# A graph layer on one core: masks moved to GpSimd as a no-edge comparison, and the pair loop put in a fixed issue order

## The chip, the cores and the metric

One core of a Trainium2 chip. The metric is the device time of one execution in microseconds (us). "Before" and "after" are the kernel before and after the change. Engines carry the names of the profile: PE is TensorE, PEld its weight loads, DVE is VectorE, ACT is ScalarE, POOL is GpSimd, SP is SyncE. The experiments ran in four batches on three chips; the kernel before, run beside each batch, had medians of 459.6 to 461.2 us.

## The reference, cut to what matters

Two graph layers over 3327 nodes with 64 features and a dense adjacency of zeros and ones. Layer 0 visits all pairs of nodes; layer 1 wants, for every edge, how many edges of the same row come after it (only the last 100 count, each with half the weight of the next).

```python
adj_att = jax.nn.sigmoid(left[:, None] + right[None, :] + b_att[0]) * adj
x_local = logmap(x[:, None, :], x[None, :, :], c)
support_t = jnp.einsum('ij,ijd->id', adj_att, x_local)
...                                     # layer 1
mask = (adj != 0).astype(support.dtype)
rank = jnp.cumsum(mask, axis=1)
deg = rank[:, -1:]
k = jnp.minimum(deg, float(MAX_NEIGH))
pos = rank - (deg - k)
w = mask * jnp.where(pos > 0, DECAY ** (k - pos), 0.0)
out = w @ support + bias
```

## The kernel before

The node axis is padded to 26 blocks of 128. A strip is 8, 8, 6 or 4 blocks of targets; for each strip the kernel runs over the 26 source blocks `j` from the last to the first, in rounds of at most 1024 columns. In a round, VectorE makes a 16-bit mask of the adjacency (`ad`), PE's triangular matmuls add it to running counters in PSUM (`pc`; SBUF and PSUM are the two memories in which the kernel's tiles lie, and its matmuls write to tiles in PSUM), and ScalarE or VectorE reads the counters out as bytes (`behind`). Beside this runs the pair work: tanh of `left + right`, the sigmoid product with `ad`, the pair matmuls into `pq`, two Gelus as a stand-in for the artanh of layer 0, the last product, and a matmul that adds the round to the strip's sums `po`.

```python
ad = work.tile([P, FMAX], F32, name="ad", bufs=4)
nc.sync.dma_start(ad[:, :span]..., adj_t[...])
mask = work.tile([P, FMAX], BF16, name="mask", bufs=3)
V.tensor_scalar(mask[:, :span], ad[:, :span], 0.0, None, op0=ALU.not_equal)
for j in js:
    now = part(mask, j)
    for f0, f1 in hv:
        if before is not None:
            T.matmul(pc[:, f0:f1], ca, before[:, f0:f1], ...)
        T.matmul(pc[:, f0:f1], cb, now[:, f0:f1], ...)
    before = now
    kept = behind(j)[:, i0 : i0 + F]
    if j % (2 if b0 == 0 else 4):
        A.activation(kept, pc[:, :F], AF.Relu)
    else:
        V.tensor_scalar(kept, pc[:, :F], 0.0, None, op0=ALU.max)
sg = work.tile([P, FMAX], F32, name="sg", bufs=3)
for j in js:
    A.activation(part(sg, j), left_b[:, :F], AF.Tanh, bias=right[:, j : j + 1], scale=0.5)
V.scalar_tensor_tensor(sg[:, :span], sg[:, :span], 1.0, ad[:, :span], op0=ALU.add, op1=ALU.mult)
pq = ps.tile([P, FMAX], F32, name="pq", bufs=2)
...                                     # pair matmuls into pq
s = work.tile([P, FMAX], F32, name="s", bufs=3)
A.activation(s[:, :span], pq[:, :span], AF.Gelu, scale=-WG / QS)
A.activation(s[:, :span], s[:, :span], AF.Gelu, scale=WH)
V.scalar_tensor_tensor(s[:, :span], s[:, :span], WD, sg[:, :span], op0=ALU.add, op1=ALU.mult)
for j in js:
    ...                                 # T.matmul(po, hw, s)
    next(steps, None)                   # one step of the per-node chain of the strip before
```

The per-node chain (`post`) closes layer 0 for the nodes of a finished strip, and it makes the rows that layer 1 multiplies. It is a row of VectorE instructions. In this kernel the order of each engine's queue is left to the scheduler.

Of the kernel before, what the change touches and what calls it, by code (L numbers as in the profile page):

```python
# [11 lines left out]
F32 = mybir.dt.float32  # L12
# [10 lines left out]
P = 128  # L23
# [5 lines left out]
STRIPS = [(0, 8), (8, 8), (16, 6), (22, 4)]  # L29
FMAX = 8 * P  # L30
JH = 13

GSTRIPS = [(0, 7), (7, 7), (14, 6), (20, 6)]
GFMAX = 7 * P
# [30 lines left out]


HS = 1024.0
CNT = 127.0


def halves(n):
# [364 lines left out]
def fast(ctx, tc, x, adj_t, r, w_att, b_att, weight, bias, out, flag):  # L436
# [27 lines left out]
    def column(value, name):  # L464
# [8 lines left out]
    id16 = const.tile([P, P], F16, name="id16")  # L473
    G.tensor_copy(id16, ident)

    cb = const.tile([P, P], BF16, name="cb")
    ca = const.tile([P, P], BF16, name="ca")
    G.memset(ca, -1.0)
    G.affine_select(out=cb, in_=ca, compare_op=ALU.is_gt, fill=0.0, base=0,
                    pattern=[[-1, P]], channel_multiplier=1)  # L480
    G.affine_select(out=cb, in_=cb, compare_op=ALU.not_equal, fill=CNT, base=0,
                    pattern=[[-1, P]], channel_multiplier=1)
    G.tensor_sub(ca, ca, cb)
    row1 = const.tile([1, P], BF16, name="row1")
    G.memset(row1, 1.0)
    rowc = const.tile([1, 512], BF16, name="rowc")
    G.memset(rowc, MAX_NEIGH - CNT)

    node = const.tile([P, NB], F32, name="node")
    G.memset(node, 1.0)  # L490
# [34 lines left out]
    behind_hi = const.tile([P, NB - JH, NP], U8, name="behind_hi")  # L525
    s2 = const.tile([P, NB, 2, D], F16, name="s2")

    post_pool = ctx.enter_context(tc.tile_pool(name="post", bufs=1))
    pairs = ctx.enter_context(ExitStack())
    ps = pairs.enter_context(tc.tile_pool(name="ps", bufs=1, space=PSUM))  # L530

    with tc.tile_pool(name="pre", bufs=1) as pre:
# [102 lines left out]
        V.tensor_mul(right, plr[:, :, 1], yr)  # L635
        V.tensor_scalar(right, right, batt, 0.5, op0=ALU.add, op1=ALU.mult)


        wn, opx = small("wn"), small("opx")
        V.tensor_scalar(wn, nrm, WA / 2, None, op0=ALU.mult)  # L640
# [16 lines left out]
    def behind(j):  # L657
        return behind_lo[:, j] if j < JH else behind_hi[:, j - JH]

    def in_range():  # L660

        st = post_pool.tile([P, 4], F32, name="st")
        t1 = post_pool.tile([P, NB], F32, name="st1")
        V.tensor_mul(t1, nrm, node)
        V.tensor_reduce(st[:, 0:1], t1, AX.X, ALU.max)
        V.scalar_tensor_tensor(t1, x2, c_c, t1, op0=ALU.mult, op1=ALU.mult)
        V.tensor_reduce(st[:, 1:2], t1, AX.X, ALU.max)
        V.tensor_mul(t1, bal, node)
        V.tensor_reduce(st[:, 2:3], t1, AX.X, ALU.max)
        V.tensor_reduce(st[:, 3:4], t1, AX.X, ALU.min)  # L670
        V.tensor_scalar(st[:, 3:4], st[:, 3:4], -1.0, None, op0=ALU.mult)
        pf = ps.tile([P, P], F32, name="pq", bufs=2)
        T.transpose(pf[:4, :], st, ident)
        st2 = post_pool.tile([4, 1], F32, name="st2")
        V.tensor_reduce(st2, pf[:4, :], AX.X, ALU.max)
        pf = ps.tile([P, P], F32, name="pq", bufs=2)
        T.transpose(pf[:1, :4], st2, ident[:4, :4])
        st3 = post_pool.tile([1, 4], F32, name="st3")
        V.tensor_copy(st3, pf[:1, :4])
        ok = post_pool.tile([1, 2], F32, name="ok")  # L680

        V.tensor_mul(ok, st3[:, 0:4:2], st3[:, 1:4:2])
        V.tensor_scalar(ok[:, 0:1], ok[:, 0:1], QMAX / 2, None, op0=ALU.is_le)
        V.tensor_scalar(ok[:, 1:2], ok[:, 1:2], 0.0, None, op0=ALU.is_equal)
        V.tensor_mul(ok[:, 0:1], ok[:, 0:1], ok[:, 1:2])
        V.tensor_scalar(flag, ok[:, 0:1], -1.0, 1.0, op0=ALU.mult, op1=ALU.add)
# [95 lines left out]
        V.tensor_sub(s2[:, bs, 1], w, s2[:, bs, 0])  # L782


    steps = iter(())
    for b0, nb in STRIPS:
        F = nb * P
        i0 = b0 * P
        hv = halves(F)
        blocks = slice(b0, b0 + nb)  # L790
        queue = nc.scalar if b0 == 0 else nc.sync

        iz = strip.tile([P, 8, P], F16, name="iz")[:, :nb]
        iu = strip.tile([KB, 8, P], F16, name="iu")[:, :nb]
        queue.dma_start(iu[:D], ju[:D, blocks])
        queue.dma_start(iu[D:], ju[KB : KB + 7, blocks])
        queue.dma_start(iz[:D], jz[D:, blocks])
        queue.dma_start(iz[D:], jz[:D, blocks])
        izf, iuf = iz.rearrange("p b q -> p (b q)"), iu.rearrange("p b q -> p (b q)")
        pc = ps.tile([P, FMAX], F32, name="pc")  # L800
        po = ps.tile([P, FMAX], F32, name="po")
        pl = ps.tile([P, FMAX], F32, name="pq", bufs=2)
        for b in range(nb):
            T.transpose(pl[:, b * P : (b + 1) * P], left[:, b0 + b : b0 + b + 1].to_broadcast([P, P]), ident)
        left_b = strip.tile([P, FMAX], F32, name="left_b", bufs=1)
        A.copy(left_b[:, :F], pl[:, :F])
        for f0, f1 in hv:
            T.matmul(pc[:, f0:f1], row1, rowc[:, : f1 - f0], start=True, stop=True, skip_group_check=True)

        per = FMAX // F  # L810
        before = None
        for hi in range(NB, 0, -per):
            lo = max(hi - per, 0)
            js = range(hi - 1, lo - 1, -1)
            span = (hi - lo) * F

            def part(t, j, a=0, b=F):
                return t[:, (j - lo) * F + a : (j - lo) * F + b]

            ad = work.tile([P, FMAX], F32, name="ad", bufs=4)  # L820
            nc.sync.dma_start(ad[:, :span].rearrange("p (b f) -> p b f", f=F),
                              adj_t[lo * P : hi * P, i0 : i0 + F].rearrange("(b p) f -> p b f", p=P))
            mask = work.tile([P, FMAX], BF16, name="mask", bufs=3)
            V.tensor_scalar(mask[:, :span], ad[:, :span], 0.0, None, op0=ALU.not_equal)  # L824
            for j in js:
                now = part(mask, j)
                for f0, f1 in hv:
                    if before is not None:
                        T.matmul(pc[:, f0:f1], ca, before[:, f0:f1], start=False, stop=True, skip_group_check=True)  # L829
                    T.matmul(pc[:, f0:f1], cb, now[:, f0:f1], start=False, stop=True, skip_group_check=True)  # L830
                before = now
                kept = behind(j)[:, i0 : i0 + F]
                if j % (2 if b0 == 0 else 4):
                    A.activation(kept, pc[:, :F], AF.Relu)  # L834
                else:
                    V.tensor_scalar(kept, pc[:, :F], 0.0, None, op0=ALU.max)  # L836


            sg = work.tile([P, FMAX], F32, name="sg", bufs=3)
            for j in js:  # L840
                A.activation(part(sg, j), left_b[:, :F], AF.Tanh, bias=right[:, j : j + 1], scale=0.5)  # L841
            V.scalar_tensor_tensor(sg[:, :span], sg[:, :span], 1.0, ad[:, :span], op0=ALU.add, op1=ALU.mult)  # L842

            pq = ps.tile([P, FMAX], F32, name="pq", bufs=2)
            for j in js:
                for f0, f1 in hv:
                    T.matmul(part(pq, j, f0, f1), ju[:KB, j, :], iuf[:, f0:f1], start=True, stop=False)  # L847
                    T.matmul(part(pq, j, f0, f1), jz[:, j, :], izf[:, f0:f1], start=False, stop=True)  # L848
            s = work.tile([P, FMAX], F32, name="s", bufs=3)
            A.activation(s[:, :span], pq[:, :span], AF.Gelu, scale=-WG / QS)  # L850
            A.activation(s[:, :span], s[:, :span], AF.Gelu, scale=WH)  # L851
            V.scalar_tensor_tensor(s[:, :span], s[:, :span], WD, sg[:, :span], op0=ALU.add, op1=ALU.mult)  # L852
            for j in js:
                for f0, f1 in hv:
                    T.matmul(po[: D + 1, f0:f1], hw[:, j, :], part(s, j, f0, f1), start=j == NB - 1, stop=j == 0)  # L855
                next(steps, None)
        for _ in steps:
            pass

        ot = work.tile([P, FMAX], F32, name="s", bufs=3)[: D + 1]  # L860
        V.tensor_copy(ot[:, :F], po[: D + 1, :F])
        pa = ps.tile([P, FMAX], F32, name="pq", bufs=2)
        for b in range(nb):
            c0 = (b // 4) * 512 + (b % 4) * (D + 1)
            T.transpose(pa[:, c0 : c0 + D + 1], ot[:, b * P : (b + 1) * P], ident[: D + 1, : D + 1])
        agg = post_pool.tile([P, 8, D + 1], F32, name="agg", bufs=2)
        for c in range(0, nb, 4):
            n = min(4, nb - c)
            A.copy(agg[:, c : c + n], pa[:, c * P : c * P + n * (D + 1)].rearrange("p (b d) -> p b d", b=n))
        steps = post(agg[:, :nb], b0, nb)  # L870
        if b0 == 0:
            in_range()
    pairs.close()


# [4 lines left out]
    with tc.tile_pool(name="l1", bufs=2) as l1, tc.tile_pool(name="l1_ps", bufs=1, space=PSUM) as l1_ps:  # L880
# [16 lines left out]
        for j in range(late):  # L897
            wt = decode(j)
            for n in range(len(chunks)):
                add(j, wt, n)  # L900
            for _ in range(2):
                next(steps, None)
        for _ in steps:
            pass
        weights = [decode(j) for j in range(late, NB)]
# [70 lines left out]
```

## Time and profile before

| | before |
|---|---|
| time, first three runs | 461.72 us median (459.25 to 464.87) |
| busy share PE, DVE, ACT, POOL | 82, 89, 80, 3 % |
| pair loop (first sigmoid to last copy of the sums) | 343.6 us of 459.1 |
| strips 0 to 3, by the prediction's cuts | 96.5, 104.1, 85.5, 57.5 us |

The lines themselves are in the prediction. Each has an engine, its line of the program, an operation, and what it wrote from what; "mean ns" is one instruction's duration, and neighbours on one engine overlap a little, so a duration of 1.22 us means one every 1.13 us. The figure after an arrow is the idle time that this releaser ended.

### The profile page before, as it was taken

What the parts mean: (1) busy time and instruction counts of PE and PEld (TensorE: products, weight loads), DVE (VectorE), ACT (ScalarE), POOL (GpSimd) and SP (SyncE); (2) the same over time, 40 slices, a digit from 0 to 9 for tenths busy, and PEclk for the clock granted to TensorE, in tenths of its full rate; (3) what the DMA queues carried; (4) which work ended last, traced back from release to release, by engine and by line L of the source; (5) the groups of instructions that cost most, each with busy time, mean ns of one, the idle gap of its engine ahead of it and who ended that gap; (6) DMA issues with size and microseconds to landing.
All of it is one profiled execution on the core that took longest, in us unless ns stands there. A gap on an engine that the chain in (4) does not pass through costs nothing.

```text
span 459.1 us, 4660 instructions
## 1 busy us (share of the span) xinstructions
PE 378.4 (82%) x1484; PEld 153.4 (33%) x1484; DVE 407.1 (89%) x774; ACT 369.2 (80%) x423; POOL 13.3 (3%) x30
## 2 busy tenths in 40 slices
PE   0266699999989799999997999889778897699293
PEld 0035233333323233333333444434322332244152
DVE  3895689999988999999998999999999998999821
ACT  1445989999894999999995999999599995888310
POOL 6000000000000000001000000020000000000000
PEclk9997699999999999999999999999999998899877
DMA  7103354545541444444442444344533420000003
GB/s 201 62 1 72 105 168 143 141 151 163 167 135 46 133 143 140 137 137 137 137 127 75 136 137 140 106 128 125 168 93 111 121 89 1 1 1 1 0 0 82
DMA packets 22840, 47.77 MB, mean 104 GB/s; under 512 B 8652, under 2 KB 9082, under 8 KB 22808
## 3 DMA queue, kind: packets, MB, share of 16 engines
q1 hardware_dynamic: 20522, 46.47, 34.7%
q10 hardware_dynamic: 2062, 0.87, 0.9%
q0 software_dynamic: 224, 0.07, 0.3%
q8 instruction: 13, 0.21, 0.2%
q14 instruction: 19, 0.16, 0.1%
HBM read 45.22 MB, written 0.85 MB: 100 GB/s over the span
## 4 chain that ended last, share of the span: by engine, by line

## 5 line engine op out<-in xcount | busy, mean ns | idle before, releaser
L855 PE MATMUL po<-s,hw 128*65 128x512 f32 (+1 forms) x364 | 165.3, 576 | 11.5 <-DVE s L852 11.1
L842 DVE SCALAR_TENSOR_TENSOR sg<-sg,ad 128x1024 f32<-128x1024 f32 (+1 forms) x91 | 103.5, 1141 | 7.5 <-ACT sg L841 7.3
L852 DVE SCALAR_TENSOR_TENSOR s<-s,sg 128x1024 f32<-128x1024 f32 (+1 forms) x91 | 104.8, 1152 | 3.7 <-ACT s L851 3.6
L841 ACT ACTIVATE sg<-left_b,right 128x1024 f32<-128x1024 f32 (+2 forms) x104 | 102.7, 1001 | 0.1
L851 ACT ACTIVATE s<-s 128x1024 f32<-128x1024 f32 (+1 forms) x91 | 91.4, 1006 | 0.1
L850 ACT ACTIVATE s<-pq 128x1024 f32<-128x1024 f32 (+1 forms) x91 | 87.7, 969 | 2.6 <-PE pq L848 2.6
L829 PE MATMUL pc<-mask,ca 128*128 128x512 bf16 (+1 forms) x175 | 65.7, 375 | 17.3 <-DVE behind_hi L836 7.2
L855 PEld LDWEIGHTS po<-s,hw 128*65 128x65 f32 x364 | 45.2, 138 | 98.9 <-issue 52.7
L847 PE MATMUL pq<-iu,ju 71*128 71x512 f16 (+1 forms) x182 | 67.8, 374 | 11.6 <-ACT s L850 11.6
L830 PE MATMUL pc<-mask,cb 128*128 128x512 bf16 (+1 forms) x182 | 66.7, 376 | 5.3 <-DVE mask L824 5.1
L848 PE MATMUL pq<-iz,jz 128*128 128x512 f16 (+1 forms) x182 | 66.6, 371 | 0.0
L824 DVE TENSOR_SCALAR mask<-ad 128x1024 bf16<-128x1024 f32 (+1 forms) x91 | 59.3, 654 | 3.4 <-PE pc L829 1.8
L894 PE MATMUL pw<-wt,s 128*128 128x512 bf16 (+1 forms) x182 | 41.0, 390 | 12.9 <-DVE s L782 9.2
L834 ACT ACTIVATE behind_hi<-pc 128x1024 uint8<-128x1024 f32 (+2 forms) x37 | 31.8, 860 | 24.3 <-PE pc L830 24.1
L830 PEld LDWEIGHTS <-cb 128*128 128x128 bf16 x182 | 17.9, 99 | 57.8 <-issue 46.6
L834 ACT ACTIVATE behind_lo<-pc 128x1024 uint8<-128x1024 f32 (+2 forms) x33 | 28.2, 853 | 7.1 <-PE pc L830 6.4
L894 PEld LDWEIGHTS <-s 128*128 128x128 f16 x182 | 18.7, 103 | 35.0 <-DVE s L782 9.6
L848 PEld LDWEIGHTS <-jz 128*128 128x128 f16 x182 | 18.1, 99 | 31.5 <-issue 15.3
L829 PEld LDWEIGHTS <-ca 128*128 128x128 bf16 x175 | 17.5, 100 | 30.8 <-issue 19.5
L847 PEld LDWEIGHTS <-ju 71*128 71x128 f16 x182 | 18.1, 100 | 21.4 <-issue 4.8
L836 DVE TENSOR_SCALAR behind_lo<-pc 128x1024 uint8<-128x1024 f32 (+2 forms) x19 | 19.9, 1050 | 1.1 <-PE pc L830 1.1
L771 POOL TENSOR_TENSOR x_sb<-x_sb,bias_b 128x512 f32<-128x512 f32 (+2 forms) x4 | 6.3, 1577 | 418.4 <-DVE w L769 418.4
(209 smaller groups left out, 290.0 us busy)
## 6 DMA issues: line engine op xcount, KB each, us to landing
ad<-in_adj_t SPq DMA_DIRECT2D x65, 512.0 KB, 3.7
ad<-in_adj_t SPq DMA_DIRECT2D x26, 384.0 KB, 3.3
out<-o SPq DMA_DIRECT2D x6, 128.0 KB, 2.0
x_sb<-in_x SPq DMA_DIRECT2D x1, 416.0 KB
x_sb<-in_x ACTq DMA_DIRECT2D x1, 416.0 KB, 6.9
iz<-jz ACTq DMA_DIRECT2D x2, 128.0 KB
iz<-jz SPq DMA_DIRECT2D x2, 128.0 KB, 2.4
iz<-jz SPq DMA_DIRECT2D x2, 96.0 KB
```

Of the source, the lines that this page charges most:

```text
L829: T.matmul(pc[:, f0:f1], ca, before[:, f0:f1], start=False, stop=True, skip_group_check=True)
L830: T.matmul(pc[:, f0:f1], cb, now[:, f0:f1], start=False, stop=True, skip_group_check=True)
L834: A.activation(kept, pc[:, :F], AF.Relu)
L841: A.activation(part(sg, j), left_b[:, :F], AF.Tanh, bias=right[:, j : j + 1], scale=0.5)
L842: V.scalar_tensor_tensor(sg[:, :span], sg[:, :span], 1.0, ad[:, :span], op0=ALU.add, op1=ALU.mult)
L847: T.matmul(part(pq, j, f0, f1), ju[:KB, j, :], iuf[:, f0:f1], start=True, stop=False)
L848: T.matmul(part(pq, j, f0, f1), jz[:, j, :], izf[:, f0:f1], start=False, stop=True)
L850: A.activation(s[:, :span], pq[:, :span], AF.Gelu, scale=-WG / QS)
L851: A.activation(s[:, :span], s[:, :span], AF.Gelu, scale=WH)
L852: V.scalar_tensor_tensor(s[:, :span], s[:, :span], WD, sg[:, :span], op0=ALU.add, op1=ALU.mult)
L855: T.matmul(po[: D + 1, f0:f1], hw[:, j, :], part(s, j, f0, f1), start=j == NB - 1, stop=j == 0)
L894: T.matmul(pw[n], s2[:, j].rearrange("p c d -> p (c d)"), wt[:, f0:f1].bitcast(BF16), start=j == 0, stop=j == NB - 1)
```

## The change

Its intent: take the 50 us of masks off the busiest engine and give them to the one that is idle; mark entries without an edge, so that the counters' start value and the zeroing of non-edges come from constants and a bias column; and put DVE, ACT and PE in one fixed order, in which the sums of a round are added two rounds later (lag two) and the counters are made three rounds ahead.

```diff
-            mask = work.tile([P, FMAX], BF16, name="mask", bufs=3)
-            V.tensor_scalar(mask[:, :span], ad[:, :span], 0.0, None, op0=ALU.not_equal)
+    def edges(n):
+        mask_of[n] = mask = work.tile([P, FMAX], BF16, name="mask", bufs=3)
+        args = mask[:, : span(n)], ad_of[n][:, : span(n)]
+        G.tensor_scalar(*args, 0.0, None, op0=ALU.is_equal)
...
-                if j % (2 if b0 == 0 else 4):
-                    A.activation(kept, pc[:, :F], AF.Relu)
-                else:
-                    V.tensor_scalar(kept, pc[:, :F], 0.0, None, op0=ALU.max)
+        rest = none[:, NB - 1 - j : NB - j]
+        if (NB - 1 - j) % den >= den - num:          # ON_ACT = ((1, 6), (2, 5), (1, 2), (1, 2))
+            A.activation(kept, S.pc[:, : S.F], AF.Relu, bias=rest)
+        else:
+            V.tensor_scalar(kept, S.pc[:, : S.F], rest, 0.0, op0=ALU.add, op1=ALU.max)
...
-            A.activation(s[:, :span], pq[:, :span], AF.Gelu, scale=-WG / QS)
-            A.activation(s[:, :span], s[:, :span], AF.Gelu, scale=WH)
-            V.scalar_tensor_tensor(s[:, :span], s[:, :span], WD, sg[:, :span], op0=ALU.add, op1=ALU.mult)
...
+    with tc.manual_schedule(engines={mybir.EngineType.DVE, mybir.EngineType.Activation, mybir.EngineType.PE}):
+        for n in range(R):
...                                                  # sums of round n - 2
+            A.activation(pq, pq, AF.Gelu, scale=-WG / QS)
+            A.activation(pq, pq, AF.Gelu, scale=WH)
+            V.scalar_tensor_tensor(sg, sg, 1.0, ad_of.pop(n)[:, :w], op0=ALU.add, op1=ALU.mult)
+            edges(m + 1)                             # m = n + 3; ends of the loop cut here
+            count(m, js(m)[-1])
+            sigmoids(n + 1)
+            read(m, js(m)[-1])
+            products(n + 1)
+            for _ in js(n):
+                next(steps, None)
...
+            V.scalar_tensor_tensor(sg, pq, WD, sg, op0=ALU.add, op1=ALU.mult)
```

Cut here: seven buffers of adjacency and five of sigmoids (4 and 3 before); `left` of strips 1 to 3 by a DMA from device memory; the range check split into steps and moved.

## The prediction

The sum came to 443 us (461.7 less 18.7 of gain). The 9 us for "lock waits", VectorE waiting while GpSimd works, were the author's estimate, and no trace gave their size. What the trace showed of such waits is the timeline of the add and the mask (2.19 us, and 1.18 instead of 0.69). "The port rival" is the first of the rivals; "port" is a name here and nothing that was shown.

> **What bounds the kernel now.** I read the page first, then the four strips of the pair loop one by one, then the groups with shapes kept apart, then the timeline. The page:
>
> ```profile
> span 459.1 us, 4660 instructions
> PE 378.4 (82%) x1484; PEld 153.4 (33%) x1484; DVE 407.1 (89%) x774; ACT 369.2 (80%) x423; POOL 13.3 (3%) x30
> ```
>
> Three engines are over 80%, GpSimd is empty. The pair loop runs from 46.7 us (first sigmoid) to 390.3 us (last copy of the sums); I cut it where a strip's sums are copied out, or where the next strip's broadcast of `left` starts. Columns of the table by windows: stretch, its length, then busy time and count of PE, PEld, DVE, ACT, POOL, granted clock, DMA share, GB/s.
>
> ```profile
> 46.70:143.20 96.50, 90.48 (x292) 31.86 (x289) 87.78 (x88) 87.74 (x91) 0.00 (x0) 0.96 0.49 145
> 143.20:247.30 104.10, 96.44 (x332) 34.36 (x332) 101.34 (x177) 97.18 (x105) 2.19 (x1) 1.00 0.44 129
> 247.30:332.80 85.50, 75.42 (x338) 34.85 (x337) 82.68 (x169) 77.85 (x108) 2.40 (x1) 1.00 0.44 126
> 332.80:390.30 57.50, 49.44 (x153) 16.33 (x151) 54.84 (x123) 51.59 (x76) 1.00 (x1) 0.97 0.28 83
> ```
>
> DVE is busy 326.6 of 343.6 us. From strip 1 on it is the bound (97% there: the per-node work of the strip before is DVE work too); in strip 0 no engine is over 94%. DMA is at half load and no bound. What DVE and ACT do in a round (mean ns, idle before):
>
> ```profile
> L852 DVE SCALAR_TENSOR_TENSOR s<-s,sg 128x1024 f32<-128x1024 f32 x65 | 79.6, 1225 | 3.7 <-ACT s L851 3.6
> L842 DVE SCALAR_TENSOR_TENSOR sg<-sg,ad 128x1024 f32<-128x1024 f32 x65 | 79.0, 1217 | 7.5 <-ACT sg L841 7.3
> L851 ACT ACTIVATE s<-s 128x1024 f32<-128x1024 f32 x65 | 69.3, 1068 | 0.1
> L850 ACT ACTIVATE s<-pq 128x1024 f32<-128x1024 f32 x65 | 66.5, 1030 | 2.6 <-PE pq L848 2.6
> L841 ACT ACTIVATE sg<-left_b,right 128x1024 f32<-128x1024 f32 x52 | 60.1, 1165 | 0.0
> L824 DVE TENSOR_SCALAR mask<-ad 128x1024 bf16<-128x1024 f32 x65 | 45.0, 695 | 3.1 <-PE pc L829 1.8 <-PE pc L830 0.7 <-DMA ad<-in_adj_t 0.6
> L836 DVE TENSOR_SCALAR behind_lo<-pc 128x1024 uint8<-128x1024 f32 x11 | 13.4, 1218 | 0.0
> ```
>
> Neighbouring instructions overlap, so I price by start-to-start distances in the timeline (DVE from 232.5 us, ACT from 234.6 us): both products and a counter read on DVE 1.13 us each, a mask 0.60; on ACT the Gelus 0.91 and 0.95, tanh 1.04, a counter read 0.90. At 768 columns: mask 0.48, product or read 0.87; a read of 512: 0.60.
>
> PE's 378 us mislead. From the timeline of one round:
>
> ```profile
> 153.27 1.88 PE L855 MATMUL po<-s,hw 128*65 128x512 f32 x4
> 154.99 0.38 PE L829 MATMUL pc<-mask,ca 128*128 128x512 bf16 x1
> 155.20 0.38 PE L830 MATMUL pc<-mask,cb 128*128 128x512 bf16 x1
> 155.42 0.38 PE L829 MATMUL pc<-mask,ca 128*128 128x512 bf16 x1
> ```
>
> A 16-bit matmul lasts 0.38 but the next starts 0.216 later; the four fp32 passes take 1.72. A 1024-column round thus costs PE 1.72 + 8 x 0.216 = 3.45 us. Strip 0 takes 96.5/26 = 3.71 a round, so PE is the next bound, close by.
>
> [...] mask 695 ns, read of PSUM at the same width 1218. So reads are dear on DVE, and moving a product's operand to PSUM should not slow it: it was at 1217 already. [...] The trace has no comparison on GpSimd, but its select of 128 columns took 330 ns and of 26 columns 208, so 1.2 ns a column. Its two-input add took 0.73 us for 256 and 1.00 for 384, so 2.1 ns[...]. [...]
>
> ```profile
> 215.38 1.22 DVE L852 SCALAR_TENSOR_TENSOR s<-s,sg 128x1024 f32<-128x1024 f32 x1
> 215.55 2.19 POOL L771 TENSOR_TENSOR x_sb<-x_sb,bias_b 128x512 f32<-128x512 f32 x1 [207.49 <-DVE w L769]
> 216.51 0.68 DVE L773 TENSOR_REDUCE t<-dt 128x8 f32<-128x512 f32 x1
> 217.11 1.18 DVE L824 TENSOR_SCALAR mask<-ad 128x1024 bf16<-128x1024 f32 x1
> ```
>
> The add, worth about 1.27 us at 512 columns, needed 2.19: it waited out the product. The reduce beside it lost nothing; the mask behind it took 1.18 instead of 0.69, until GpSimd was done at 217.74.
>
> **The change part by part.**
> - Masks leave DVE: 15.0 us in strip 0 (25 x 0.60), 16.2 in strip 1, 12.5 in strip 2, 6.0 in strip 3; 49.7 in the loop, some 2.5 more ahead of it.
> - GpSimd gets 91 masks. At 1.2 ns a column one of 1024 takes about 0.2 + 1.2 = 1.4 us (estimate[...]), some 120 us of 344. Masks are made a round or more ahead of their counters, so GpSimd's duration alone is not on the path.
> - Counter reads move to DVE. Before, DVE reads 13 + 7 + 7 + 7; the new fractions give 22 + 16 + 13 + 13. In the windows: +11 x 1.13 = 12.4, +9 x 1.13 = 10.2, +6 x 0.87 = 5.2, +6 x 0.60 = 3.6; together 31.4 us back on DVE. ACT loses 18 x 0.90 + 6 x 0.69 + 6 x 0.48 = 23 us and three copies of `left`, which come by DMA.
> - DVE by strip: 85.2; 95.3; 75.4; 52.4. ACT falls to about 2.9 to 3.3 us per 1024-column round, under both others. PE keeps all pair matmuls: 26 x 3.45 = 89.7 in strip 0, so PE bounds there; in strip 1 the same 89.7 is below DVE.
> - Sum of bounds: 89.7 + 95.3 + 75.4 + 52.4 = 312.8 against 343.6 measured, at most 31 us off.
> - Gelu in place in PSUM: saves buffers, and takes the second SBUF input from the last product[...]. ACT is off the path, so I count no time.
> - Fixed order, lag two, counters three rounds ahead: removes waits at strip changes (1.5 to 4 us of idle each on DVE or ACT around 245 to 250 us) and the counter chain at the end, where ACT waited 1.43 and 1.73 us for counters. About 1.5 us at the drain.
> - Range check: its reductions go into the loop, its short transposes into the last stage, where DVE was busy 43.8 of 46.6 us and the per-node chain holds the end: about +2.
> - Ahead of the loop: 4 to 5 masks fewer on DVE, about one read more, one transpose and a store more: about -1.
>
> I don't expect all of the 31 us. DVE idled 5% of the loop; with three engines again within 10% of each other and queues in fixed order I keep half of it, 8 us. [...] Then 343.6 - 312.8 - 8 - 9 = 14 us of gain, 18 if the strip changes overlap as planned. With -1, -1.5 and +2 that stays about 18: 461.7 - 18.7 = 443.
>
> **The rivals.**
> - [...] The sigmoid product (1.13 us a round) and most per-node products still have two SBUF inputs. If a mask starts just ahead of the product every time, DVE waits up to 1.4 us a round; a mean of 0.4 over 91 rounds is 36 us: 465 to 480. For it: the 1.18 us mask above. Against: a mask's buffer is freed by the counters' matmuls, just ahead of the read of PSUM[...]; GpSimd then runs beside read and last product, and has two rounds of slack.
> - *The comparison is slow on GpSimd.* At the 2.1 ns of two inputs it takes 2.4 us; with 1.13 locked by the product that nearly fills a 3.5 us round: 455 to 465. The select's 1.2 ns speaks against it.
> - *PE becomes the bound everywhere, or its clock is cut.* Then strips 0 and 1 stay at 3.45 or more: 440 to 450. It was granted 0.96 to 1.00 in the loop at 85% issue.
> - *The fixed order runs nearly stall-free.* Sum of bounds plus 5 us: 430 to 435.
>
> **Range and chances.** 443 us; the range 428 to 458 goes from the stall-free case to one where lock waits take some 25 us. Faster by over 2% is below 452.5: 0.74. Within 2%: 0.20. Slower needs the port rival at full size: 0.06.
>
> **What would show it right or wrong.** Right: no mask on DVE; GpSimd busy 100 to 150 us[...]; strip 0 near 3.5 us a round with PE nearly gapless; the sigmoid product's mean at most 1.35 us, the last product's at 1.22; DVE busy near 320 us in the loop. The port rival shows as a sigmoid product of 1.5 us or more; slow masks as GpSimd means over 2.2 us with PE waiting for masks; a bad order as DVE or ACT idle waiting for PE each round. Wrong altogether if the loop does not shrink below 335 us.

## More of the kernel before

The per-node chain (`post`) closes layer 0 for the nodes of a finished strip, and it makes the rows that layer 1 multiplies. It is a long row of small VectorE instructions of 4 to 8 columns, each needing the one before, with some of 512 columns between. Its inverse square root alone is twelve of them:

```python
def rsqrt(pool, y, v, n):
    ...
    V.tensor_scalar(t.bitcast(I32), v.bitcast(I32), 1, None, op0=ALU.logical_shift_right)
    V.tensor_scalar(y.bitcast(I32), t.bitcast(I32), -1.0, float(0x5F3759DF), op0=ALU.mult, op1=ALU.add)
    V.tensor_scalar(g, v, -0.5, None, op0=ALU.mult)
    for _ in range(3):
        V.tensor_mul(t, y, y)
        V.tensor_mul(t, t, g)
        V.scalar_tensor_tensor(y, t, 1.5, y, op0=ALU.add, op1=ALU.mult)
```

## The result, and the profile after

| | before | after |
|---|---|---|
| time, median of 4 fast runs | 460.49 us (458.78 to 464.87) | 490.94 us (489.73 to 491.46) |
| ratio to before | | 1.064, 95% interval 1.056 to 1.072 |
| first sigmoid to last copy of the sums | 343.6 us | 370.9 us |

A ratio is the mean time of one kernel's fast runs over that of the other's in the same rounds, so not quite the ratio of the medians quoted here. Executions over 1.5% slower than the fastest of the same kernel are left out of the means. The change is slower by 6%; 443 us was predicted.

The page of the kernel after, span and busy time of each engine:

```profile
span 488.0 us, 4830 instructions
...
PE 376.5 (77%) x1442; PEld 157.1 (32%) x1460; DVE 421.6 (86%) x714; ACT 356.3 (73%) x390; POOL 265.2 (54%) x121
```

VectorE lost 50 us of masks, got some 31 us of reads, and is busier than before by 15 us: 421.6 against 407.1. GpSimd took 265 us, where the prediction had 100 to 150. The strips of the kernel after, cut as in the prediction (stretch, length, busy time and count of PE, PEld, DVE, ACT, POOL, granted clock, DMA share, GB/s):

```profile
49.30:145.50 96.20, 93.09 (x316) 35.30 (x320) 92.22 (x86) 90.64 (x90) 82.47 (x27) 0.98 0.52 156
145.50:259.50 114.00, 96.16 (x320) 35.02 (x322) 107.82 (x152) 92.47 (x99) 75.46 (x29) 0.97 0.41 118
259.50:356.40 96.90, 76.98 (x313) 34.84 (x316) 88.17 (x152) 76.71 (x102) 64.84 (x28) 0.95 0.41 116
356.40:420.20 63.80, 47.71 (x134) 16.43 (x134) 53.16 (x117) 43.47 (x60) 20.73 (x8) 0.89 0.14 41
```

Strip 0 is what it was. Strips 1, 2 and 3, in which the per-node chain runs too, are 10, 11 and 6 us longer. In strip 1 DVE is busy 107.8 us where 95.3 was predicted; in strip 3 it is busy 53 of 64 us, so there it waits. Now the groups, with shapes kept apart:

```profile
L863 POOL TENSOR_SCALAR mask<-ad 128x1024 bf16<-128x1024 f32 x65 | 194.7, 3000 | 90.8 <-PE pc L874 60.5 <-issue 11.6 <-DMA ad<-in_adj_t 7.8
...
L967 DVE SCALAR_TENSOR_TENSOR sg<-sg,ad 128x1024 f32<-128x1024 f32 x65 | 85.1, 1310 | 4.8 <-DMA left_b<-left_d 4.5 <-ACT sg L894 0.3
L987 DVE SCALAR_TENSOR_TENSOR sg<-pq,sg 128x1024 f32<-128x1024 f32 x65 | 79.1, 1217 | 1.5 <-ACT pq L964 0.8
...
L901 PE MATMUL pq<-iu,ju 71*128 71x512 f16 x156 | 63.3, 406 | 30.9 <-DVE sg L987 30.2 <-issue 0.2
...
L887 DVE TENSOR_SCALAR behind_hi<-pc,none 128x1024 uint8<-128x1024 f32 x20 | 25.6, 1279 | 2.7 <-PE pc L875 2.5 <-ACT pq L964 0.2
```

Four readings. A mask is 3.0 us on average, not 1.4; between 66.8 and 84.1 us GpSimd is busy 17.29 of 17.30 us, one mask to each round of PE. The sigmoid product (L967, two inputs in SBUF) is 1310 instead of 1217; the last product (L987, one input now in PSUM) is 1217, as predicted. A read with the bias column is 1279 instead of 1218. And PE waits 30 us for the last product before the next pair matmuls; before, its wait there was another, and a third as long. The waits of the kernel after (total, times, longest us), then that of the kernel before:

```profile
PE pq L901 <- DVE sg L987: 30.2, 25, 3.4
...
ACT pq L963 <- PE pq L902: 20.2, 34, 2.2
...
ACT k L745 <- DVE t L744: 10.5, 3, 5.8
```

```profile
PE pq L847 <- ACT s L850: 11.6, 14, 3.1
```

Two things in the timeline explain these lines. **First, held instructions.** The timeline of the kernel after: start, duration, engine, instruction.

```profile
170.56 2.77 POOL L863 TENSOR_SCALAR mask<-ad 128x1024 bf16<-128x1024 f32 x1 [0.18 <-PE pc L874]
170.61 2.07 DVE L967 SCALAR_TENSOR_TENSOR sg<-sg,ad 128x1024 f32<-128x1024 f32 x1
172.60 1.27 DVE L887 TENSOR_SCALAR behind_hi<-pc,none 128x1024 uint8<-128x1024 f32 x1
```

```profile
208.21 2.77 POOL L863 TENSOR_SCALAR mask<-ad 128x1024 bf16<-128x1024 f32 x1 [1.76 <-PE pc L874]
208.31 0.95 DVE L516 SCALAR_TENSOR_TENSOR rn<-rs_t,rn 128x8 f32<-128x8 f32 x1
...
209.90 1.10 DVE L775 TENSOR_SCALAR rn<-rn,maxnorm 128x8 f32<-128x8 f32 x1
```

The product that starts just behind a mask takes 2.07 us instead of 1.22, but it ends at 172.68, while the mask runs until 173.33. It was held for 0.85 us, not for the whole mask. (Spans on POOL are rough, but two masks back to back in this trace start 2.75 us apart, so 2.77 stands.) An instruction of 8 columns is held in the same way: 0.95 us instead of 0.17. A TENSOR_SCALAR of 8 columns, SBUF to SBUF, is held to the end of the mask: both end near 211.0. I added up, over all DVE instructions, what each took beyond the usual duration of its form ("stretch" from here on): 3.1 us before, 26.7 after; of these 11.8 fall on SCALAR_TENSOR_TENSOR (the sigmoid product above all), 7.9 on TENSOR_TENSOR and 7.0 on TENSOR_SCALAR. What is called usual moves these sums a little: a recount with the median of each form in its own trace gives 3.6 and 27.1.

**Second, the queue.** The kernel after, DVE, ACT and PE around one inverse square root:

```profile
178.30 0.17 DVE L511 TENSOR_SCALAR rn<-rs_t 128x8 int32<-128x8 int32 x1
...
178.71 0.17 DVE L515 TENSOR_TENSOR rs_t<-rs_t,rs_g 128x8 f32<-128x8 f32 x1
178.91 0.17 DVE L516 SCALAR_TENSOR_TENSOR rn<-rs_t,rn 128x8 f32<-128x8 f32 x1
179.11 0.17 DVE L514 TENSOR_TENSOR rs_t<-rn 128x8 f32<-128x8 f32 x1
...
179.51 0.95 DVE L516 SCALAR_TENSOR_TENSOR rn<-rs_t,rn 128x8 f32<-128x8 f32 x1
...
181.41 0.23 DVE L744 SCALAR_TENSOR_TENSOR t<-t,sqc,t 128x8 f32<-128x8 f32 x1
181.56 1.22 DVE L987 SCALAR_TENSOR_TENSOR sg<-pq,sg 128x1024 f32<-128x1024 f32 x1
181.67 0.21 ACT L745 ACTIVATE k<-t 128x8 f32<-128x8 f32 x1 [5.80 <-DVE t L744]
...
182.83 0.61 PE L901 MATMUL pq<-iu,ju 71*128 71x512 f16 x1 [3.35 <-DVE sg L987]
```

From 178.11 to 181.56 DVE does nothing but the chain, a dependent instruction every 0.20 us, and the last product of the round stands behind it. One link, at 179.51, is itself held by a mask (0.95 us), so about 0.8 of these 3.45 us belong to the first cause. ACT waits 5.8 us, because its next function in the fixed order is the chain's tanh, and PE waits 3.35 us for the product. Behind this wait PE is slower too: the matmul at 182.83 lasts 0.61 us. In the loop 40 of 588 counter and pair matmuls of 512 columns last over 0.45 us instead of 0.38 (10 of 600 before), and what follows them starts 8.0 us later in sum (1.8 before). The same chain in the kernel before:

```profile
182.52 0.16 DVE L734 TENSOR_TENSOR y<-u,k 128x8 f32<-128x8 f32 x1
182.60 0.16 DVE L736 TENSOR_TENSOR xy<-xy,k 128x8 f32<-128x8 f32 x1
182.68 1.22 DVE L852 SCALAR_TENSOR_TENSOR s<-s,sg 128x1024 f32<-128x1024 f32 x1
183.81 0.16 DVE L735 TENSOR_TENSOR y<-y,k 128x8 f32<-128x8 f32 x1
```

Here the scheduler puts a product between two dependent small instructions; independent neighbours follow each other in 0.08 us. In strip 1 the small instructions (26 columns or fewer written; each counted to its end or to the next start) occupy 9.8 us of DVE before (77 of them, 128 ns each) and 15.6 after (70, 223 ns each).

### The profile page after: what moved, and what is told of

It reads as the page before. It is cut to its first block, busy times and chain, and to the rows that moved or that the text cites. A ratio compares the mean times of both kernels' runs of the same rounds, so it can differ in the third digit from the quotient of the medians.

```text
span 488.0 us, 4830 instructions
## 1 busy us (share of the span) xinstructions
PE 376.5 (77%) x1442; PEld 157.1 (32%) x1460; DVE 421.6 (86%) x714; ACT 356.3 (73%) x390; POOL 265.2 (54%) x121
## 4 chain that ended last, share of the span: by engine, by line
## 5 line engine op out<-in xcount | busy, mean ns | idle before, releaser
L863 POOL TENSOR_SCALAR mask<-ad 128x1024 bf16<-128x1024 f32 (+1 forms) x91 | 254.2, 2798 | 127.6 <-PE pc L874 69.9
L911 PE MATMUL po<-sg,hw 128*65 128x512 f32 (+1 forms) x364 | 166.8, 583 | 3.7 <-DVE sg L987 3.1
L967 DVE SCALAR_TENSOR_TENSOR sg<-sg,ad 128x1024 f32<-128x1024 f32 (+1 forms) x91 | 112.5, 1237 | 4.8 <-DMA left_b<-left_d 4.5
L987 DVE SCALAR_TENSOR_TENSOR sg<-pq,sg 128x1024 f32<-128x1024 f32 (+1 forms) x91 | 103.8, 1141 | 2.2 <-ACT pq L964 1.3
L963 ACT ACTIVATE pq<-pq 128x1024 f32<-128x1024 f32 (+1 forms) x91 | 86.5, 951 | 22.9 <-PE pq L902 20.2
L964 ACT ACTIVATE pq<-pq 128x1024 f32<-128x1024 f32 (+1 forms) x91 | 86.2, 947 | 2.9
L874 PE MATMUL pc<-mask,ca 128*128 128x512 bf16 (+1 forms) x164 | 62.3, 380 | 26.7 <-DVE behind_hi L887 12.7
L875 PE MATMUL pc<-mask,cb 128*128 128x512 bf16 (+1 forms) x179 | 67.0, 384 | 14.6 <-POOL mask L863 12.6
L911 PEld LDWEIGHTS po<-sg,hw 128*65 128x65 f32 x364 | 51.3, 143 | 78.6 <-issue 59.9
L887 DVE TENSOR_SCALAR behind_hi<-pc,none 128x1024 uint8<-128x1024 f32 (+2 forms) x34 | 37.9, 1115 | 8.5 <-PE pc L875 8.3
L887 DVE TENSOR_SCALAR behind_lo<-pc,none 128x1024 uint8<-128x1024 f32 (+2 forms) x30 | 33.5, 1117 | 4.6 <-ACT pq L964 1.7
L901 PEld LDWEIGHTS <-ju 71*128 71x128 f16 x182 | 18.5, 102 | 49.3 <-DVE sg L987 30.1
L902 PEld LDWEIGHTS <-jz 128*128 128x128 f16 x182 | 18.6, 102 | 31.9 <-issue 16.8
L1015 PEld LDWEIGHTS <-s 128*128 128x128 f16 x182 | 18.4, 102 | 31.9 <-DVE s L797 9.4
L885 ACT ACTIVATE behind_lo<-pc,none 128x1024 uint8<-128x1024 f32 (+2 forms) x22 | 19.9, 903 | 11.2 <-PE pc L875 7.0
```

What stands on the lines that cost most here:

```text
L863: G.tensor_scalar(*args, 0.0, None, op0=ALU.is_equal)
L874: T.matmul(S.pc[:, f0:f1], ca, S.before[:, f0:f1], start=False, stop=True, skip_group_check=True)
L875: T.matmul(S.pc[:, f0:f1], cb, now[:, f0:f1], start=S.first, stop=True, skip_group_check=True)
L887: V.tensor_scalar(kept, S.pc[:, : S.F], rest, 0.0, op0=ALU.add, op1=ALU.max)
L901: T.matmul(part(n, pq, j, f0, f1), ju[:KB, j, :], S.iu[:, f0:f1], start=True, stop=False)
L902: T.matmul(part(n, pq, j, f0, f1), jz[:, j, :], S.iz[:, f0:f1], start=False, stop=True)
```

## The experiments

**Theory.** Two causes of similar size: GpSimd's reading of SBUF holds up DVE (P), and the fixed order lets large instructions stand behind the chain (O). **Rivals.** GpSimd is too slow and masks come late; the counter reads moved to DVE are what costs; the PSUM buffers of the pair matmuls, now held until the last product, are what costs. Fifteen kernels were run (nothing is on record under e9). Medians of the fast runs, in us:

| label | kernel | time | ratio to before |
|---|---|---|---|
| e1_fill | after, masks filled with ones (wrong result) | 472.0 | 1.023 |
| e2_dve | after, masks on DVE | 507.4 | 1.101 |
| e3_before_pool | before, masks on GpSimd | 489.5 | 1.062 |
| e4_free_order | after, order left to the scheduler | 464.5 | 1.007 |
| e5_slow_fill | as e1, filled three times (wrong) | 478.0 | 1.039 |
| e6_fine | after, chain cut finer | 487.0 | 1.056 |
| e7_fill_free | e1 and e4 together (wrong) | 440.1 | 0.956 |
| e8_fine_fill | e1 and e6 together (wrong) | 458.6 | 0.995 |
| e10_before_pool_psum | e3, Gelus in place in PSUM | 503.9 | 1.094 |
| e11_no_masks | before without masks | 448.9 | 0.974 |
| e12_after_no_masks | after without masks, free order | 437.5 | 0.948 |
| e13_half | after, half of each mask compared (wrong) | 481.1 | 1.041 |
| e14_fixed | e12 in the fixed order | 473.2 | 1.026 |
| e15_fixed_sbuf | e14, Gelus into SBUF | 469.2 | 1.016 |
| e16_free_sbuf | e12, Gelus into SBUF | 433.1 | 0.941 |

### Each half of the change undone

```diff
-        G.tensor_scalar(*args, 0.0, None, op0=ALU.is_equal)
+        G.memset(args[0], 1.0)                                                  # e1_fill
+        V.tensor_scalar(*args, 0.0, None, op0=ALU.is_equal)                     # e2_dve
```
```diff
-            V.tensor_scalar(mask[:, :span], ad[:, :span], 0.0, None, op0=ALU.not_equal)
+            G.tensor_scalar(mask[:, :span], ad[:, :span], 0.0, None, op0=ALU.is_gt)   # e3_before_pool, in the kernel before
```
```diff
-    with tc.manual_schedule(engines={mybir.EngineType.DVE, mybir.EngineType.Activation, mybir.EngineType.PE}):
+    with ExitStack():                                                           # e4_free_order
```

e1_fill keeps every mask instruction in its place, but GpSimd now writes without reading, no longer waits for the adjacency, and is faster (953 ns a mask); the counters come out wrong. e3 compares with "greater than" where the kernel before has "not equal"; for zeros and ones it is the same.

> The changed kernel with GpSimd filling each mask with a constant instead of comparing (wrong result on purpose): GpSimd no longer reads SBUF[...]. Theory P[...]: the 25 us by which VectorE instructions are stretched in the changed kernel's trace go, and some waiting with them: 455 to 468 us. Theory O (the fixed issue order: per-node chains back to back, rounds of uneven length): the time stays at 480 to 490 us.

Measured: 472.0 us (471.1 to 474.7, four fast runs; the fifth, 479.7, was slow), 18.9 less than after; with the slow run the median is 472.4, from which later expectations reckon. The stretch fell from 26.7 to 4.0 us, its part on SCALAR_TENSOR_TENSOR from 11.8 to 1.4.

> The changed kernel, fixed order and all, with the same comparison on VectorE again. It gives VectorE 50 us of masks[...]. Theory P: the move of the masks was worth only 50 - 25 = 25 us or less, so 500 to 515 us. Theory O: the move as such was worth nearly the 50 us and the order lost them again: 525 to 540 us.

Measured: 507.4 us (504.5 to 509.1). Within the fixed order, moving the masks to GpSimd is a gain of 16 us; with masks on DVE the fixed order is far behind the kernel before. This is no price of the order alone, since the counter reads that the change moved stay on DVE too.

> The kernel before with its masks on GpSimd (greater than zero, the same for this 0 or 1 matrix) and nothing else changed: one part alone, in the scheduler's own order. Theory P: 50 us leave VectorE, 25 come back[...], and ScalarE, which still has most counter reads, limits: 445 to 458 us, or even no gain. Theory O: 430 to 445 us, a clear gain, since the masks' move is good and only the order is bad.

Measured: 489.5 us (487.8 to 492.0), 29 us slower than before, from this move alone. Its stretch is 51 us (48 in the recount): about what DVE lost in masks came back in longer instructions, and DVE is busy 409.2 us as against 407.1 before. The lines of e3_before_pool, mask and last product:

```profile
L824 POOL TENSOR_SCALAR mask<-ad 128x1024 bf16<-128x1024 f32 x65 | 195.1, 3009 | 103.1 <-DMA ad<-in_adj_t 49.9 <-PE pc L829 42.1 <-remote 4.6
...
L852 DVE SCALAR_TENSOR_TENSOR s<-s,sg 128x1024 f32<-128x1024 f32 x65 | 92.5, 1424 | 11.1 <-ACT s L851 11.0
```

The last product has two inputs in SBUF here, and it is 1424 ns instead of 1225.

> The changed kernel without the fixed issue order: the same instructions, but VectorE, ScalarE and TensorE ordered by the scheduler as in the kernel before. Theory P: GpSimd still reads 91 times, so within 10 us of 491. Theory O: the order's share comes back, 450 to 465 us.

Measured: 464.5 us (463.4 to 465.2), 26.5 less than after, and within 1% of the kernel before. Its stretch is 35 us, more than in the fixed order, and yet it is faster: the order and GpSimd's reads are two causes. The free order also starts later (first sigmoid at 55.7 us instead of 49.3): four counter reads now stand between 33.0 and 49.5 us, amid the chain that leads to the loop. So the near tie with the kernel before hides two things. From the first sigmoid to the last copy e4 takes 332.0 us, 11.6 less than before; outside the loop it takes 131 us, 16 more; part of that is work moved behind the loop, where DVE does 149 instructions instead of 110.

### Reading or duration, chain or order

```diff
-        G.tensor_scalar(*args, 0.0, None, op0=ALU.is_equal)
+        for _ in range(3):
+            G.memset(args[0], 1.0)                                              # e5_slow_fill
```
```diff
-        rsqrt(pool, rn, t0, nb)
+        yield from rsqrt_steps(pool, rn, t0, nb)      # as rsqrt, with a yield after each link (e6_fine)
...                                                    # more yields in the rest of the chain, a few instructions moved by a place
+    def slot(n):                                      # called after edges() and after the last product as well
+        for _ in js(n):
+            next(steps, None)
```

e5_slow_fill occupies GpSimd for as long as the comparison (about 2.8 us a mask) without reading SBUF. e6_fine spreads the chain through the round and keeps the rest of the fixed order. e7 and e8 are the two edits with e1's fill.

> As the fill run (472 us), but each mask filled three times over, about 2.8 us of GpSimd as long as a comparison, still without reading SBUF (wrong result on purpose). If GpSimd's reads are what costs[...]: 470 to 476 us. If its duration costs (masks late[...]): 480 to 491 us.

Measured: 478.0 us (474.8 to 480.7), 6.0 more than the quick fill in the medians, with profiled spans of 473.6 and 472.9. Its runs fall in two pairs, 475 us at a granted clock of 0.95 and 480.6 at 0.92; the first is 3 us above the quick fill. Of the 18.9 us that e1 gains, most is what GpSimd reads and not how long it works. The rest may be spread, or the TENSOR_SCALARs, which are stretched by 7.6 us in e5 and 2.5 in e1 (recount): no run separates the two.

> The changed kernel with masks on GpSimd and the fixed order, but the per-node chains cut fine (each Newton step of the reciprocal root a step of its own) and handed out at three places of a round instead of one. If the order's share is the chains that stand back to back on VectorE: 468 to 480 us. If it is something else in the order (lag two, counters ahead, places of the reads): 488 to 494 us.

Measured: 487.0 us (485.8 to 487.7), only 4 less than after.

> Both taken away: scheduler's order and masks filled (wrong result on purpose). If the two causes add, 491 - 18.5 - 26.5 = 446 us, 440 to 452. If they are one cause seen twice[...]: 458 to 466 us.

Measured: 440.1 us (439.6 to 441.3). Without reading and without the order, the kernel is near the predicted 443, but that sum had allowed 17 us for these two losses (below). The counter reads stay on DVE here, so they are not what makes the change slow.

> The finely cut fixed order with masks filled (wrong result on purpose). If the chains are the order's share[...]: 445 to 458 us, near the run with both taken away. If the chains are not it: 468 to 474 us like the fill run.

Measured: 458.6 us (457.6 to 458.8), 13.5 less than e1_fill. So cutting the chain finer is worth 13.5 us where GpSimd does not read, and 4 where it does. The traces say why: spread over the round, the chain's small instructions meet masks more often. In strip 1 the 70 small instructions occupy 10.4 us in e8 (149 ns each) and 22.0 us in e6 (314 ns each), and the whole stretch is 5.1 us in e8 and 36.5 in e6. What the finer chain gives, the longer instructions take back.

### A second SBUF input taken away, and half a mask

```diff
-            A.activation(s[:, :span], pq[:, :span], AF.Gelu, scale=-WG / QS)
-            A.activation(s[:, :span], s[:, :span], AF.Gelu, scale=WH)
-            V.scalar_tensor_tensor(s[:, :span], s[:, :span], WD, sg[:, :span], op0=ALU.add, op1=ALU.mult)
+            A.activation(pq[:, :span], pq[:, :span], AF.Gelu, scale=-WG / QS)   # e10, on top of e3
+            A.activation(pq[:, :span], pq[:, :span], AF.Gelu, scale=WH)
+            V.scalar_tensor_tensor(s[:, :span], pq[:, :span], WD, sg[:, :span], op0=ALU.add, op1=ALU.mult)
```
```diff
+        half = span(n) // 2                                                     # e13_half
-        G.tensor_scalar(*args, 0.0, None, op0=ALU.is_equal)
+        G.tensor_scalar(args[0][:, :half], args[1][:, :half], 0.0, None, op0=ALU.is_equal)
+        G.memset(args[0][:, half:], 1.0)
```

> The kernel before with its masks on GpSimd and, besides, both Gelus in place in PSUM, so that the last product of a round has one input in SBUF and one in PSUM. Theory[...]: the last product is no longer stretched, its mean falls from about 1.37 us to 1.22, the stretch of VectorE instructions falls from 51 us to some 25, and the time from 489.5 us to about 470. Rival (what costs is that masks come late, or the queue order): the last product's input makes no difference, 485 to 492 us.

Measured: 503.9 us (503.2 to 505.0): the expectation for the time failed, by 34 us and in its sign. What it said of VectorE's instructions held: the stretch fell from 51 to 22 us and the last product to 1220 ns. The lines of e10_before_pool_psum, last product and first Gelu:

```profile
L852 DVE SCALAR_TENSOR_TENSOR s<-pq,sg 128x1024 f32<-128x1024 f32 x65 | 79.2, 1220 | 23.1 <-ACT pq L851 22.9
...
L850 ACT ACTIVATE pq<-pq 128x1024 f32<-128x1024 f32 x65 | 65.7, 1012 | 27.2 <-PE pq L848 27.2
```

The first Gelu waits 27 us for the pair matmuls (7 in e3), and the last product 23 us for the Gelus (11 in e3). A PSUM buffer `pq` that the first Gelu used to free is now held until the last product, and there are two. That is the likely source of these waits; this run alone does not separate it from the new order that the scheduler chose.

> The changed kernel in its fixed order; GpSimd compares the first half of each round's columns and fills the second half with ones (wrong result on purpose). Theory (what GpSimd reads is what holds VectorE up, for a time that grows with the columns read): a two-input product that starts with the mask is held for about 0.46 us after the mask's start instead of 0.90, the stretch of VectorE instructions falls from 26.7 us to 10 to 16, and the time is half way between the fill's 472 and the 491 of the changed kernel, 480 to 484 us. Rival (any comparison costs the same, however short): 487 us or more.

Measured: 481.1 us (476.5 to 481.9), half way between fill and comparison, with 9.2 us of stretch, just under the expected range. The timeline of e13_half, a mask of 512 columns and a product close behind it:

```profile
157.82 1.50 POOL L864 TENSOR_SCALAR mask<-ad 128x512 bf16<-128x512 f32 x1 [1.49 <-issue]
157.87 1.64 DVE L969 SCALAR_TENSOR_TENSOR sg<-sg,ad 128x1024 f32<-128x1024 f32 x1
```

The product, worth 1.215 us, was free to run 0.47 us after the mask's start (1.642 - 1.215 + 0.047). For products that began just behind an undisturbed mask this point is 0.90 us at 1024 columns (nine cases, 0.894 to 0.901), 0.68 at 768 (seven), 0.47 at 512 and 0.37 at 384 (two each or more, in this run). Hence a fixed part and some 0.83 ns a column, a third of the mask's own 2.5 ns a column (1.18 us at 384, 2.77 at 1024). It is no limit: a mask can itself be held by a two-input product before it, and then lets the next two-input instruction go later by the same amount. In the kernel after, the mask at 167.11 us, 0.56 us behind the start of such a product, lasts 3.27 us, 0.50 more than undisturbed, and frees the next one (L730, 512 columns, 1.52 us instead of 0.68) after 1.41 us, 0.51 more. In these runs the cost goes with what GpSimd reads: a stretch of 4.0 us with fills (e1), 9.2 with half of each mask compared, 26.7 with all of it.

### No masks at all

The counters' matmuls can read the adjacency directly. It is 32-bit floating point, and for a zero or a one the upper 16 bits are the same number in bf16:

```diff
-        mask_of[n] = mask = work.tile([P, FMAX], BF16, name="mask", bufs=3)
-        args = mask[:, : span(n)], ad_of[n][:, : span(n)]
-        G.tensor_scalar(*args, 0.0, None, op0=ALU.is_equal)
+        mask_of[n] = ad_of[n].bitcast(BF16).rearrange("p (f t) -> p f t", t=2)[:, :, 1]
```

This marks edges, so the signs of the counters' constants `ca` and `cb` are turned in e12, and its reads need no bias column. It is right for an adjacency of zeros and ones, as the reference makes it, and not for other weights: a kernel for those would need a check and another path. e11_no_masks does the same to the kernel before (five buffers of adjacency, every second counter read by DVE in all strips).

> The kernel before without any mask instruction: the counters' matmuls read the upper half of each 32-bit entry of the adjacency, which for an entry of 0 or 1 is 0 or 1 in bf16, and VectorE reads the counters of every second block in all strips. Correct for an adjacency of zeros and ones. Theory (VectorE's 50 us of masks were worth removing, the way of removing them was not): bounds of 89.7 us of TensorE in strip 0, some 92, 76 and 52 us in the others give 310 us of loop, with the kernel before's own 15 us of losses 325, in all about 441 us. Rival (TensorE takes a 16-bit operand with a stride of 4 bytes at half rate): 8 counter matmuls of a round last 0.43 us each instead of 0.216, a round 5.2 us, over 500 us.

Measured: 448.9 us (448.1 to 449.4), correct, 8 us above the expectation. With the reads moved, the 50 us of masks were worth 12 us to the kernel before. Strip 1 takes 104 us as before: from 179 to 215 us PE, ACT and DVE are all busy 11.6 to 12.0 of every 12 us, so no single one can be named as its bound, and at the strip's change PE is busy only 5.3 of the last 8.4 us.

> The changed kernel in free order without any mask instruction: counters from the upper halves of the adjacency's entries, the counters' constants with their signs turned, so that reads need no bias column. Correct for an adjacency of zeros and ones. Theory: as with the fill in free order (440 us, wrong result), less some 4 us because a read on VectorE costs 1.13 us from start to start again instead of 1.20: 436 us. Rival (TensorE slows with the stride): over 470 us.

Measured: 437.5 us (436.1 to 438.6), correct. The stride of 4 bytes costs PE little; the timeline of e12_after_no_masks:

```profile
200.53 0.39 PE L871 MATMUL pc<-ad,ca 128*128 128x512 bf16 x1
200.75 0.39 PE L872 MATMUL pc<-ad,cb 128*128 128x512 bf16 x1
```

They follow each other in 0.225 to 0.227 us in most cases, as against 0.216 with packed masks: some 10 ns more, or about 4 us of PE over the 358 counter matmuls (an estimate from these two spacings). The expected rival, 0.43 us each, did not come.

### The fixed order, and the PSUM buffers

These three were run because e10 and PE's wait for the last product pointed at the held PSUM buffers. e14 is e12 with the fixed order put back. e15 and e16 give the Gelus a buffer in SBUF again, so that the first Gelu frees `pq`:

```diff
-            A.activation(pq, pq, AF.Gelu, scale=-WG / QS)
-            A.activation(pq, pq, AF.Gelu, scale=WH)
+            s_of[n] = work.tile([P, FMAX], F32, name="s", bufs=4)
+            s = s_of[n][:, :w]
+            A.activation(s, pq, AF.Gelu, scale=-WG / QS)
+            A.activation(s, s, AF.Gelu, scale=WH)
...
-            V.scalar_tensor_tensor(sg, pq, WD, sg, op0=ALU.add, op1=ALU.mult)
+            V.scalar_tensor_tensor(s, s, WD, sg, op0=ALU.add, op1=ALU.mult)
```

> The changed kernel without masks (counters from the upper halves of the adjacency's entries) in its fixed order; correct for an adjacency of zeros and ones. Against the free order's 437.5 us it gives the price of the fixed order where GpSimd does nothing in the loop. From the fill in the two orders (472 and 440 us) I expect the same 25 to 32 us: 463 to 469 us. If the fill's own writes made the difference: below 455 us.

Measured: 473.2 us (471.7 to 473.8): the fixed order costs 36 us where GpSimd does nothing in the loop. Cut at each strip's copy of its sums (columns as above), first e14_fixed, strips 1 to 3:

```profile
145.90:250.20 104.30, 93.44 (x321) 34.34 (x319) 97.70 (x153) 91.47 (x99) 1.29 (x1) 0.98 0.42 129
250.20:340.90 90.70, 78.14 (x319) 34.88 (x320) 80.19 (x152) 75.10 (x101) 1.29 (x1) 0.94 0.42 123
340.90:404.50 63.60, 46.67 (x132) 15.87 (x130) 50.42 (x116) 41.63 (x59) 1.00 (x1) 0.89 0.13 39
```

Then e12_after_no_masks, the same strips:

```profile
147.70:241.00 93.30, 90.42 (x317) 34.41 (x318) 91.51 (x150) 88.92 (x98) 1.28 (x1) 1.00 0.47 137
241.00:316.60 75.60, 72.08 (x314) 33.19 (x315) 74.25 (x147) 73.87 (x102) 1.28 (x1) 1.00 0.50 148
316.60:359.70 43.10, 40.72 (x131) 14.68 (x134) 41.54 (x87) 39.06 (x57) 0.00 (x0) 1.00 0.16 48
```

In free order DVE is busy 98, 98 and 96% of the strips: they sit on their bound, and the bounds are close to those predicted for strips 1 and 2 (95.3 and 75.4). In the fixed order the same work takes 11, 15 and 20 us more; strip 0, which has no chain, differs by 1 (98.3 and 97.2, from the first sigmoid). Small instructions take 184 ns against 129 in strip 1, and DVE, PE and ACT all wait. PE's wait for the last product in strips 1 to 3, e14 and then e12:

```profile
PE pq L897 <- DVE sg L983: 18.6, 19, 2.4
```

```profile
PE pq L897 <- DVE sg L983: 2.5, 4, 1.2
```

Some of strip 3's gain is only moved: its DVE did 87 instructions instead of 116, and the part after the loop is 77.2 us in e12 and 67.0 in e14. The first sigmoid comes at 50.5 and 47.6 us. So the loop alone is 48 us longer in the fixed order, and 12 of them come back outside it.

> As e14_fixed, but both Gelus write a buffer in SBUF, as in the kernel before, so that the first Gelu frees the PSUM buffer of the pair matmuls and not the last product (three buffers of sigmoids, six of adjacency, four of Gelus). Theory that the fixed order is dear because the PSUM buffer is held until the last product, which stands behind the per-node chain in VectorE's queue: TensorE's wait of 23 to 30 us for that product goes, 440 to 452 us. Rival, that the order is dear because TensorE's last matmul and ScalarE's functions wait for the queue whoever holds the buffer: within 6 us of e14_fixed.

Measured: 469.2 us (465.7 to 470.6), 4 less than e14. The PSUM buffers are not what makes the fixed order dear: my theory for this run fell, its rival held.

> As e15_fixed_sbuf in free order. With the buffer freed early and the order free, both theories say no better than a few us under the free order's 437.5 us with Gelus in PSUM: 432 to 440 us. Above 445 us would say that fewer buffers of sigmoids and adjacency cost more than the early release brings.

Measured: 433.1 us (432.5 to 434.0), correct, and the best of all: 6% faster than the kernel before (ratio 0.941, interval 0.935 to 0.946) and 12% than the change. The Gelus' own buffer in SBUF, and with it the early release of `pq`, is worth 4 us in either order.

## Why the prediction was wrong

**What held.** The sum of bounds, 312.8 us for the loop: e12 takes 309.2 (97.2 + 93.3 + 75.6 + 43.1), with part of strip 3 moved behind it. In the steady part of strip 0 the kernel after runs at PE's 3.45 us a round, gapless, as predicted. No mask is left on DVE, and the last product is at 1217 ns. The sigmoid product's mean, 1.31 us, is within the 1.35 named. Without the two causes below the kernel took 440 us (e7, wrong result) and 437 (e12, correct). That these are near 443 is luck: the sum had allowed 8 + 9 = 17 us for the two, so its own figure without them is 426. The loop is not what misses it. Outside the loop e7 and e12 take 129 and 128 us where the kernel before takes 115.5 and the prediction had 0.5 us less. The sum also rests on the larger of its two gains, 18 us and not 14.

**The failed step, first: "removes waits at strip changes", and of the idle time "I keep half of it, 8 us".** This is the largest error. The fixed order adds 26 us with masks on GpSimd (e4), 32 with fills (e1 and e7), 36 without masks (e14 and e12). The diff showed one reason: all steps of the chain that fall in a round stand in one place, ahead of the last product. I priced a fixed queue by what it removes and never laid out one round of it, with dependent instructions at 0.20 us, to see what stands behind what. The signature that I named, DVE or ACT idle waiting for PE each round, was turned round: PE waits for DVE, and ACT for both. The sign "wrong altogether" came: the loop grew to 370.9 us. No time was put to a bad order, and "slower" was given 0.06, by the first rival alone. Finer steps give 14 us of the 32 (e8). The other 18 were not split further; the difference lies in strips 1 to 3, and PE and ACT waits behind the chain are still in its trace.

**Second: "one of 1024 takes about 0.2 + 1.2 = 1.4 us".** It takes 2.77 undisturbed, 3.0 on average. I took a select's rate for a comparison's. The rival with slow masks came nearer (2.4 us), and masks do fill PE's round in part of strip 0, but it did not have the way in which they cost: PE waits for a mask once, 12.6 us ahead of the loop, and a filler of the same length is only 1 to 6 us slower than a quick one.

**Third, a size: the 9 us for lock waits.** Such waits came, though a two-input product is held until 0.90 us after the mask's start and not for the mask's 2.77 us; their size is 18 to 19 us in the fixed order (after 490.9, e14 473.2, e1 472.0), some 24 to 27 in the free one (464.5 against 440.1 and 437.5). The first rival put all of it on the sigmoid product, 1.5 us or more; it is at 1.31. Over half of the stretch is elsewhere, on the chain's small and wide instructions, which I mentioned and did not price. A small one, worth 0.17 us, was held for up to 0.93 us.

**Small terms.** A read with a bias column comes every 1.20 us instead of 1.13: 38 of 1024 columns, 2.7 us. "Gelu in place ... I count no time": it costs 4 us (e16 against e12), probably by the PSUM buffer held longer; the numbers of buffers differ too.

**The sum.** 426 us without the two losses; e7, without them, took 440, so 14 us lie outside the two, nearly all outside the loop as above. From e7 to the kernel after the two cost 51 us: 24.4 for reading and then 26.5 for the order (by e4), or 31.9 for the order and then 18.9 for reading (by e1). They are not quite independent: each taken alone from the kernel after is worth 18.9 and 26.5, 45.4 together. 17 of the 51 had been allowed: 443 + 14 + 51 - 17 = 491.

**Why the change alone is slower than the kernel before.** DVE's masks were worth less than their 50 us: without them the kernel before is at 449 (e11). GpSimd masks in the kernel before are a loss in themselves, 29 us (e3), and the fixed order costs 26 to 36 us in every pair that differs in it alone. Only the new structure in free order, with masks that cost DVE nothing, shows what the rebalancing is worth: 437.

## What to carry to other kernels

Before you move work to GpSimd, count the VectorE instructions that can be held by it, small ones too: here one of 0.17 us took 0.95 or 1.10, and finer interleaving gave such holds more chances (in strip 1, 314 ns a small instruction in e6, 149 with fills in e8). Before you fix an issue order, write one round out with durations and ask what stands behind the longest dependent chain; a chain of tiny dependent instructions wants large independent ones between its links (in strip 1, 129 ns a small instruction in e12's free order, 184 in e14's fixed one). And look for a form in which the work isn't needed: a view of bits that were already there beat the best place for the instruction.
